# A fused cross-attention kernel: one operand sum moved from an accumulating DMA to VectorE, and operand loads asked for in another half of the period

## The chip, the cores and the metric

The kernel runs on one core of one Trainium2 chip. The time is the device time of one execution in microseconds (us); the median over executions is what counts. Everything is float32.

## The reference

For each of 8 batches, with `x1` and `x2` (the context) of 512 channels by 1024 positions:

```
q = x1^T Wq + bq          # 1024 x 64
k = Wk x2 + bk            # 64 x 1024
v = Wv x2 + bv            # 512 x 1024
attn = softmax(q k, over the 1024 context positions)
out = v attn^T + x1       # 512 x 1024
```

## The kernel before

**The algebra.** The kernel computes `out = Wv (x2 attn^T) + bv + x1`: it first forms `y = x2 E` with E the exponentials of the scores, then `o = Wv y`. Both products are done by a seven-product (Strassen-Winograd) scheme over 2 x 2 blocks. The left blocks of `y` are A11, A12, A21, A22 (`s.a["11"]` and so on: 128 partitions x 4 x 256, 512 KB each, loaded from a transposed copy of `x2`). Their sums are S1 = A21 + A22, S2 = A11 - S1, S3 = A11 - A21, S4 = A12 + S2. The right blocks are halves of E (`s.t["11"]` and so on, 128 x 4 x 512); T1 = E12 - E11, T2 = T1 - E22, T3 = E22 - E12, T4 = E21 + T2. The table `MULT` says which left and right operand product 1 to 7 takes: product 3 is S4 x E22, product 4 is A22 x T4, product 7 is S3 x T3. Some of these products are split once more by the same scheme: `inner_left` and `inner_right` make the inner sums on VectorE (lines 385 and 397), `inner_product` issues four 128x256 matmuls for each of the seven inner products (line 404).

**The stages.** The whole order is written by hand (`manual_schedule`): every engine and every DMA queue runs its instructions in the order of the Python program. `period(s, n, nn, nnn)` is called once for each batch b = 0 to 7 and is called "period b" here; `n`, `nn`, `nnn` are the next three batches. Its first half makes y of batch b: products 1, 2, 6, then the scores of `n` (first half of the positions) and the queries of `nn`, then products 5, 7, 3, the other scores of `n` and the keys of `nn`, and product 4. Its second half makes o of batch b (seven products against the weights) and, beside it on VectorE, the softmax of `n` and the sums S1, S2, S3 of `n`. Batches 2 to 7 are `late`; batches 2 to 5 and 7 (`seven`) split product 7 as well.

**How three sums are made in late periods.** VectorE makes T1 and T2 in two halves each. T3 (`sum_t3`) is made by ScalarE and DMA: ScalarE negates E12 in place (line 285), and an accumulating DMA on POOL's queue adds E22 (line 286), in two DMAs of 512 KB. T4 (`sum_t4`) is copied on ScalarE and accumulated by two DMAs of POOL's queue (line 280). S4 (`sum_s4`) is loaded again from A12's place in HBM by a DMA of SP's queue (line 291), and an accumulating DMA of POOL's queue adds S2 (line 292). POOL issues T3, T4 and S4 in that order, behind a partition all-reduce (line 226). S4 is read first by `inner_left(s, 3, ...)` on VectorE, which stands behind `inner_right(s, 7, ...)` (it reads T3) and, where there is a next batch, the four `lower` subtractions (line 249). In periods 0 and 1 VectorE makes S4 and T3 with `tensor_tensor`.

**Where loads stand.** `load_a` issues loads of A blocks on SP's queue; A11 and A12 have one buffer each, A21 and A22 two. S3 overwrites A21, and the inner sums of product 4 take A12's buffer (tag `a12`), those of the next batch's product 2 take S4's (tag `aS4`). In each period SP's queue has, in order: A11 of `n` (after product 1), S4's load, A21 and A22 of `n`, the four pieces of `x2` of `nn` (after the queries), the four of `x1` of `nnn` (after the keys), A12 of `n` (after product 4), and four stores of the output, each of which waits for an accumulating DMA of POOL's queue (line 569).

Of the kernel before, what the change touches and what calls it, by code (L numbers as in the profile page):

```python
# [9 lines left out]
F32 = mybir.dt.float32  # L10
AF = mybir.ActivationFunctionType
ALU = mybir.AluOpType
# [3 lines left out]
def kernel(  # L16
# [47 lines left out]
    nc = tc.nc  # L64
    P = 128
    B, C, N = x1.shape
# [3 lines left out]
    MH = N // P // 2  # L70
# [4 lines left out]
    sb = ctx.enter_context(tc.tile_pool(name="sb", bufs=1))  # L75
# [25 lines left out]
    def left_sums(a, *ks):  # L101

        for k in ks:
            x, y, op = {
                "S1": ("21", "22", ALU.add),
                "S2": ("11", "S1", ALU.subtract),
                "S3": ("11", "21", ALU.subtract),
                "S4": ("12", "S2", ALU.add),
            }[k]
            nc.vector.tensor_tensor(a["21" if k == "S3" else k], a[x], a[y], op)  # L110
            if k == "S3":
                a["S3"] = a["21"]
# [9 lines left out]
    def load_x(s, x):  # L122

        s.x = sb.tile([P, CT, N], F32, tag="x", name=f"x_{s.b}_{x.tensor.name}")
        for c in range(CT):
            nc.sync.dma_start(s.x[:, c, :], x[s.b, ts(c, P), :])

    def load_a(s, *ks):
        for k in ks:
            s.a[k] = sb.tile(  # L130
                [P, MH, C // 2], F32, tag=f"a{k}", name=f"a{k}_{s.b}", bufs=1 + (k[0] == "2")
            )
            nc.sync.dma_start(s.a[k], x2T[s.b, int(k[0]) - 1, int(k[1]) - 1])

    def sum_a(s, *ks):
        for k in ks:
            if k != "S3":
                s.a[k] = sb.tile([P, MH, C // 2], F32, tag=f"a{k}", name=f"a{k}_{s.b}")
        left_sums(s.a, *ks)

    def project(s, nm, w_sb, bank=None):

        if bank:
            ps = ps_a.tile([P, H], F32, tag=bank, name=f"ps_{nm}_{s.b}")
        else:
            ps = ps_s.tile([P, 2, H], F32, tag="sc", name=f"ps_{nm}_{s.b}")[:, 0, :]
        for c in range(CT):
            for h, r in ((0, lo), (1, hi)):
                nc.tensor.matmul(  # L149
                    ps[r, :],  # L150
                    w_sb[:, c, :],
                    s.x[:, c, ts(h, H)],
                    start=(c == 0),
                    stop=(c == CT - 1),
                )
        return ps
# [12 lines left out]
    def keys(s, bank=None):  # L169

        ps = project(s, "k", wk_sb, bank)
        s.k = sb.tile([P, H], F32, tag="k", name=f"k_{s.b}", bufs=2)
        nc.scalar.activation(s.k, ps, AF.Identity, bias=bk_sb)

    def scores(s, h, i, bank=None):


        if i == 0:
            s.e[h] = sb.tile([P, 2, MH, H], F32, tag=f"e{h}", name=f"e_{s.b}_{h}")
        e = s.e[h]  # L180
        if bank:
            whole = None
            ps = [
                ps_a.tile([P, H], F32, tag=f"{bank}{g}", name=f"ps_s{bank}{g}_{s.b}_{h}_{i}")
                for g in range(2)
            ]
        else:
            whole = ps_s.tile([P, 2, H], F32, tag="sc", name=f"ps_s_{s.b}_{h}_{i}")
            ps = [whole[:, g, :] for g in range(2)]
        for g, r in ((0, lo), (1, hi)):  # L190
            nc.tensor.matmul(  # L191
                ps[g], s.k[r, ts(i, P)], s.q[r, ts(h, H)], start=True, stop=True
            )

        def copy():
            if bank:
                for g in range(2):
                    nc.scalar.copy(e[:, g, i, :], ps[g])
            else:
                nc.scalar.copy(e[:, :, i, :], whole)  # L200

        copy.ps = ps
        return copy
# [19 lines left out]
    def total(s, h):  # L223
        fold_halves(s, h, ALU.add)
        s.den[h] = sb.tile([P, H], F32, tag="den", name=f"den_{s.b}_{h}", bufs=2)
        nc.gpsimd.partition_all_reduce(s.den[h], s.mx[h][:, 0, :], P, ReduceOp.add)  # L226
        s.few[h] = sb.tile([P, H // P], F32, tag="few", name=f"few_{s.b}_{h}", bufs=2)
        nc.gpsimd.dma_start(
            s.few[h], s.den[h][0:1, :].rearrange("o (p f) -> o p f", p=P)
        )  # L230
# [28 lines left out]
    def right_sums(t, k):  # L259

        x, y = {"T1": ("12", "11"), "T2": ("T1", "22"), "T3": ("22", "12"), "T4": ("21", "T2")}[k]
        nc.vector.tensor_tensor(t[k], t[x], t[y], ALU.add if k == "T4" else ALU.subtract)
# [8 lines left out]
    def sum_t4(s):  # L271

        s.t["T4"] = t4 = sb.tile([P, MH, H], F32, tag="eT4", name=f"eT4_{s.b}")
        if s.b < 2:
            sum_e(s, "T4")
            return
        for i in (0, 2):
            nc.scalar.copy(t4[:, i : i + 2, :], s.t["21"][:, i : i + 2, :])
        for i in (0, 2):
            nc.gpsimd.dma_start(t4[:, i : i + 2, :], s.t["T2"][:, i : i + 2, :], accum_op=ALU.add)  # L280

    def sum_t3(s, i):
# [1 line left out]
        t3 = s.t["T3"][:, i : i + 2, :]  # L284
        nc.scalar.mul(t3, t3, -1.0)
        nc.gpsimd.dma_start(t3, s.t["22"][:, i : i + 2, :], accum_op=ALU.add)

    def sum_s4(s):

        s.a["S4"] = sb.tile([P, MH, C // 2], F32, tag="aS4", name=f"aS4_{s.b}")  # L290
        nc.sync.dma_start(s.a["S4"], x2T[s.b, 0, 1])
        nc.gpsimd.dma_start(s.a["S4"], s.a["S2"], accum_op=ALU.add)

    def copy_u1(s, j):
        if j == 0:
# [3 lines left out]
    def sum_e(s, *ks, of=(0, 2)):  # L299
        for i in of:  # L300
            part = {n: v[:, i : i + 2, :] for n, v in s.t.items()}
            for k in ks:
                right_sums(part, k)
# [75 lines left out]
    def inner_left(s, i, x, tag):  # L379

        v = {f"{p + 1}{q + 1}": x[:, ts(q, MH // 2), ts(p, P)] for p in range(2) for q in range(2)}
        sums = sb.tile([P, 4, MH // 2, P], F32, tag=tag, name=f"aI{i}_{s.b}")
        for z, (k, x, y, op) in enumerate(LEFT):
            v[k] = sums[:, z]
            nc.vector.tensor_tensor(v[k], v[x], v[y], op)  # L385
        s.inner[i] = v
# [118 lines left out]
    def evict_y(s, k, steps=(1, 2)):  # L505

        bank, add = RESULT[k]
        rden = s.rden.get(int(k[1]) - 1)
        if 1 in steps:
            s.y[k] = sb.tile([P, 2, H], F32, tag=f"y{k}", name=f"y{k}_{s.b}")  # L510
        y = s.y[k]
        for step in steps:
            for j in range(2):
                if step == 1:
                    nc.vector.tensor_tensor(y[:, j, :], s.bank[bank, j], s.tmp[add][:, j, :], ALU.add)  # L515
                else:
                    nc.vector.tensor_tensor(y[:, j, :], y[:, j, :], rden, ALU.mult)  # L517
# [198 lines left out]
    def scores_and(n, h, bank, project):  # L716


        for i in range(MH):
            scores(n, h, i, bank if i == 2 else None)()  # L720
        project()
# [4 lines left out]
    def period(s, n, nn, nnn):  # L726
# [3 lines left out]
        late = s.b >= 2  # L730
        seven = late and (s.b < B - 2 or n is None)

        def first(i, hook=None):
            multiply(s, "y", i, s.a, s.t, MH, hook=hook)
# [24 lines left out]
        else:  # L759
            sum_e(s, "T1", "T2")  # L760
            total(s, 0)
        if n:
            load_a(n, "11")
        if s.b == 0:
            first(2)
            evict_y(s, "11", (1,))
            keys(n)
            load_x(nn, x1)
            sum_t4(s)
            sums(s, 1)  # L770
            shares(s, 0)
            sum_e(s, "T3")
        else:
            complete_2 = multiply_seeded(
                s,
                2,
                "y22",
                {5: lambda: copy_u1(s, 0), 4: lambda: copy_u1(s, 1)} if late else {},
            )
            if late:  # L780
                sum_t3(s, 0)
                sum_t3(s, 2)
            else:
                sums(s, 1)
            complete_2()
            evict_y(s, "11", (1,))
            if s.b == 1:
                shares(s, 0)
            sum_t4(s)
            if late:  # L790
                sum_s4(s)
            else:
                sum_a(s, "S4")
                sum_e(s, "T3")
        if n:
            load_a(n, "21", "22")
        first(6)
        if s.b == 1:
# [2 lines left out]
        if seven:  # L801
            inner_left(s, 7, s.a["S3"], "yT4")
        if late:
            inner_left(s, 4, s.a["22"], "a12")
            evict_y(s, "11", (2,))

# [73 lines left out]
        if s.b == 1:  # L880
            inner_left(s, 4, s.a["22"], "a12")
        if n:
            scores_and(n, 1, "a", nothing)
            if s.b == 0:
                exponential(n, 0, 0)
            if nn:
                next_keys()
# [12 lines left out]
            start_sum(n, 0)  # L900
        if n:
            load_a(n, "12")
        evict_y(s, "21")
        if s.b and n:
            total(n, 0)
# [80 lines left out]
```

## Time and profile before

| | |
|---|---|
| runs | 704.22, 706.20, 707.53 us; median 706.2 |
| the profiled execution | 712.57 us; span from first to last instruction 710.4 us |
| TensorE (PE) | busy 688.5 us, 2324 matmuls, mean granted clock 0.99 |
| VectorE (DVE) | busy 606.9 us |
| ScalarE (ACT) | busy 306.1 us |
| GpSimd (POOL) | busy 230.4 us |
| DMA | 121.62 MB; POOL's queue 45.69 MB (36.0% of 16 engines' span), SP's queue 73.28 MB (28.8%) |

In the timelines a line has start, duration, engine, source line, operation, output and inputs, and in brackets the time for which the engine sat idle before it and what ended that wait. `a`, `aS`, `aI` are blocks of A, their sums, and inner sums; `e`, `eT`, `eI7yT` are E, the T sums, and the right inner sums of product 7; `ps_i3third` is the PSUM tile of an inner product of product 3. T3 shows as `e<-e` where a DMA makes it, S4 as `aS<-aS`. The profiled execution took 6.4 us more than the median of the runs.

Periods overlap by design. The start of the keys' matmuls (line 149) marks them: 170.1 us in period 1, 260.0 in period 2, 345.2 in period 3, 431.2 in period 4, 517.9 in period 5. Period 6 has no such matmuls, and period 7 ends the program.

### The profile page before, as it was taken

How to read it: one execution, taken by the hardware profiler on the slowest of the kernel's cores; microseconds unless marked ns; L12 is line 12 of the kernel's file. 1: busy time of each engine (PE TensorE's matmuls, PEld its weight loads, DVE VectorE, ACT ScalarE, POOL GpSimd, SP SyncE). 2: the span in 40 equal slices, each digit the busy share in tenths (PEclk: the TensorE clock that was granted, in tenths of full speed). 3: DMA queues.
4: the chain of work that ended last, by engine and by line, in shares of the span. 5: the costliest groups of instructions: out<-in, count | busy, mean ns of one | idle time of the engine just before them, and what ended most of it. 6: DMA issues, size and time to landing. Idle time of an engine off the chain costs nothing.

```text
span 710.4 us, 6908 instructions
## 1 busy us (share of the span) xinstructions
PE 688.5 (97%) x2324; PEld 381.0 (54%) x2324; DVE 606.9 (85%) x788; ACT 306.1 (43%) x502; POOL 230.4 (32%) x165
## 2 busy tenths in 40 slices
PE   9999999999999899999999999999899999999897
PEld 5333554546464565646547465473654745564663
DVE  1999998987999598987899778997799968997584
ACT  2733344254436444365443553444535454434120
POOL 0133114512424216342272612725127242424100
PEclk9999999999999989999999999999999999999899
DMA  9676157856388963899619987189743895279603
GB/s 308 240 246 226 32 178 146 240 159 133 109 171 241 251 125 116 162 260 262 171 50 204 260 229 208 28 198 267 205 88 49 207 251 106 49 169 250 136 0 118
DMA packets 48179, 121.62 MB, mean 171 GB/s; under 512 B 5265, under 2 KB 7569, under 8 KB 48145
## 3 DMA queue, kind: packets, MB, share of 16 engines
q0 software_dynamic: 20016, 45.69, 36.0%
q1 hardware_dynamic: 26720, 73.28, 28.8%
q10 hardware_dynamic: 1408, 2.23, 0.9%
q8 instruction: 18, 0.29, 0.2%
q14 instruction: 17, 0.13, 0.1%
HBM read 75.76 MB, written 16.81 MB: 130 GB/s over the span
## 4 chain that ended last, share of the span: by engine, by line
PE 38%; DVE 29%; DMA 22%; POOL 5%; issue 4%; SPq 1%; ACT 0%; DVEq 0%; POOLq 0%
DMA aS<-aS 14%; PE ps_ya L340 6%; PE ps_oa L340 4%; DVE aI L385 3%; DMA row<-few 3%; DVE aS L110 3%; DVE e L249 3%; PE ps_oc L340 3%; PE ps_yc L404 3%; PE ps_k L149 3%; PE ps_i4chain L404 3%; PE ps_s L191 2%; POOL den L226 2%; PE ps_ya L404 2%; DVE uo L566 2%
## 5 line engine op out<-in xcount | busy, mean ns | idle before, releaser
L340 PE MATMUL ps_ya<-eT,aS 128*128 128x512 f32 x256 | 113.1, 595 | 0.0
L226 POOL PARTITION_ALL_REDUCE den<-sum x16 | 86.1, 5381 | 49.4 <-DVE sum L215 44.4
L340 PEld LDWEIGHTS ps_ya<-eT,aS 128*128 128x128 f32 x256 | 48.0, 190 | 60.9 <-issue 58.0
L249 DVE TENSOR_TENSOR e<-e,top 128x1024 f32<-128x1024 f32 x60 | 69.4, 1217 | 3.6 <-POOL top L221 3.6
L253 ACT ACTIVATE e<-e 128x1024 f32<-128x1024 f32 x60 | 62.4, 1059 | 18.8 <-DVE e L249 17.9
L221 POOL PARTITION_ALL_REDUCE top<-max x16 | 31.4, 1960 | 120.5 <-DVE max L215 71.0
L340 PE MATMUL ps_oa<-yT,w_S 128*128 128x512 f32 x128 | 57.6, 593 | 0.0
L200 ACT COPY e<-ps_s 128x1024 f32<-128x1024 f32 x46 | 45.6, 1026 | 19.1 <-PE ps_s L191 17.5
L351 ACT COPY uy<-ps_ya 128x512 f32<-128x512 f32 x36 | 21.0, 587 | 64.7 <-PE ps_ya L340 55.6
L191 PE MATMUL ps_s<-q,k 64*128 64x512 f32 x188 | 47.3, 608 | 0.8 <-ACT q L608 0.8
L238 POOL DMA_DIRECT2D den<-row x16 | 8.9, 559 | 119.7 <-DMA row<-few 119.7
L573 POOL DMA_DIRECT2D sum<-e x21 | 25.8, 1228 | 60.9 <-DMA sum<-e 20.4
L517 DVE TENSOR_TENSOR y<-y,den 128x512 f32<-128x512 f32 x64 | 40.3, 685 | 4.5 <-DMA den<-row 4.4
L340 PEld LDWEIGHTS ps_oa<-yT,w_S 128*128 128x128 f32 x128 | 24.2, 190 | 30.8 <-issue 29.2
L211 DVE TENSOR_TENSOR max<-max,e 128x1024 f32<-128x1024 f32 x30 | 36.7, 1225 | 3.0
L569 POOL DMA_DIRECT2D uo<-in_x_dram x14 | 16.5, 1176 | 54.9 <-DVE few L234 28.0
L351 ACT COPY uo<-ps_oa 128x512 f32<-128x512 f32 x32 | 18.4, 586 | 32.3 <-PE ps_oa L340 31.3
L515 DVE TENSOR_TENSOR y<-ps_yc,uy 128x512 f32<-128x512 f32 x48 | 30.7, 681 | 0.0
L191 PEld LDWEIGHTS ps_s<-q,k 64*128 64x128 f32 x188 | 16.7, 186 | 24.6 <-issue 18.4
L340 PE MATMUL ps_oa<-y,w_S 128*128 128x512 f32 (+1 forms) x68 | 28.8, 567 | 0.0
L360 PE MATMUL ps_o<-y,w 128*128 128x512 f32 x64 | 28.8, 592 | 0.0
L340 PE MATMUL ps_o<-y,w 128*128 128x512 f32 x64 | 28.8, 592 | 0.0
(175 smaller groups left out, 1424.4 us busy)
## 6 DMA issues: line engine op xcount, KB each, us to landing
x_in_x_dram<-in_x_dram SPq DMA_DIRECT2D x60, 512.0 KB, 7.0
a<-in_x2T_dram SPq DMA_DIRECT2D x32, 512.0 KB, 7.7
sum<-e POOLq DMA_DIRECT2D x21, 512.0 KB, 5.2
r<-in_x_dram POOLq DMA_DIRECT2D x14, 512.0 KB, 6.9
uo<-in_x_dram POOLq DMA_DIRECT2D x14, 512.0 KB, 7.7
out_dram<-r SPq DMA_DIRECT2D x14, 512.0 KB, 5.4
out_dram<-uo SPq DMA_DIRECT2D x14, 512.0 KB, 4.6
e<-e POOLq DMA_DIRECT2D x12, 512.0 KB, 8.6
```

The costliest lines, as they stand in the source:

```text
L191: nc.tensor.matmul(ps[g], s.k[r, ts(i, P)], s.q[r, ts(h, H)], start=True, stop=True)
L200: nc.scalar.copy(e[:, :, i, :], whole)
L211: nc.vector.tensor_tensor(f, e[:, :, 0, :] if i == 1 else f, e[:, :, i, :], op)
L221: nc.gpsimd.partition_all_reduce(s.top[h], s.mx[h][:, 0, :], P, ReduceOp.max)
L226: nc.gpsimd.partition_all_reduce(s.den[h], s.mx[h][:, 0, :], P, ReduceOp.add)
L249: nc.vector.tensor_tensor(e, e, top, ALU.subtract)
L253: nc.scalar.activation(e, e, AF.Exp)
L340: nc.tensor.matmul(ps[:, n], left[ka][:, k, ts(j, P)], right[kb][:, k, n], start=opens and k == 0, stop=i in (2, 3, 4) and k == n_k - 1, s ...
L351: nc.scalar.copy(s.tmp[i][:, j, :], ps)
L404: nc.tensor.matmul(ps, s.inner[i][ka][:, k, :], s.inner[i, "t"][kb][:, k, :], start=opens and k == 0, stop=z in (2, 3, 4) and k == MH // 2 ...
L515: nc.vector.tensor_tensor(y[:, j, :], s.bank[bank, j], s.tmp[add][:, j, :], ALU.add)
L517: nc.vector.tensor_tensor(y[:, j, :], y[:, j, :], rden, ALU.mult)
```

## The change

- In late periods VectorE makes S4 = A12 + S2 with one `tensor_tensor`, placed behind the left inner sums of product 7 and ahead of those of product 4. `sum_s4` goes, with its load on SP's queue and its accumulating DMA on POOL's.
- In period 7, T3 is made by VectorE in two `tensor_tensor` instructions, behind T4; its two ScalarE multiplications and two accumulating DMAs go. Periods 2 to 6 keep `sum_t3`.
- A11 of the next batch is loaded behind product 3's evictions, so behind the `x2` pieces in SP's queue, in periods 1 to 6. A21 and A22 are loaded at the end of product 4 for the batch after the next, behind A12 of the next; so A21 and A22 of batches 2 to 7 are asked for most of a period earlier. Period 0 still loads batch 1's blocks where it did.

```diff
@@ -284,12 +284,6 @@
-
-    def sum_s4(s):
-
-        s.a["S4"] = sb.tile([P, MH, C // 2], F32, tag="aS4", name=f"aS4_{s.b}")
-        nc.sync.dma_start(s.a["S4"], x2T[s.b, 0, 1])
-        nc.gpsimd.dma_start(s.a["S4"], s.a["S2"], accum_op=ALU.add)
@@ -759,9 +753,8 @@
             sum_e(s, "T1", "T2")
             total(s, 0)
-        if n:
+        if s.b == 0:
             load_a(n, "11")
-        if s.b == 0:
             first(2)
@@ -777,22 +770,21 @@
-            if late:
+            if late and n:
                 sum_t3(s, 0)
                 sum_t3(s, 2)
-            else:
+            elif not late:
                 sums(s, 1)
             complete_2()
             evict_y(s, "11", (1,))
             if s.b == 1:
                 shares(s, 0)
             sum_t4(s)
-            if late:
-                sum_s4(s)
-            else:
+            if not late:
                 sum_a(s, "S4")
+            if not late or n is None:
                 sum_e(s, "T3")
-        if n:
+        if s.b == 0:
             load_a(n, "21", "22")
         first(6)
@@ -801,6 +793,7 @@
         if seven:
             inner_left(s, 7, s.a["S3"], "yT4")
         if late:
+            sum_a(s, "S4")
             inner_left(s, 4, s.a["22"], "a12")
             evict_y(s, "11", (2,))
@@ -880,6 +873,8 @@
         if n:
+            if s.b:
+                load_a(n, "11")
             scores_and(n, 1, "a", nothing)
@@ -900,6 +895,8 @@
         if n:
             load_a(n, "12")
+        if nn:
+            load_a(nn, "21", "22")
         evict_y(s, "21")
```

## The prediction

> **What bounds the kernel now.** I read the page, then VectorE's waits, then the timelines around them. TensorE is busy for 97% of the span, so the gain to be had lies in its few idle or slow microseconds. The page's engine shares, and the chain of work that ended last:
>
> ```profile
> PE 688.5 (97%) x2324; PEld 381.0 (54%) x2324; DVE 606.9 (85%) x788; ACT 306.1 (43%) x502; POOL 230.4 (32%) x165
> ...
> PE 38%; DVE 29%; DMA 22%; POOL 5%; issue 4%; SPq 1%; ACT 0%; DVEq 0%; POOLq 0%
> DMA aS<-aS 14%; PE ps_ya L340 6%; PE ps_oa L340 4%; DVE aI L385 3%; DMA row<-few 3%; DVE aS L110 3%; DVE e L249 3%; PE ps_oc L340 3%; PE ps_yc L404 3%; PE ps_k L149 3%; PE ps_i4chain L404 3%; PE ps_s L191 2%; POOL den L226 2%; PE ps_ya L404 2%; DVE uo L566 2%
> ```
>
> The largest piece of the chain is S4's accumulating DMA. VectorE's waits (total, times, longest) name it too, and behind it T3's:
>
> ```profile
> DVE aI L385 <- DMA aS<-aS: 23.5, 6, 4.7
> ...
> DVE eI7yT L397 <- DMA e<-e: 12.0, 5, 5.4
> ```
>
> Period 4 on VectorE: T3 ends a wait of 1.45 us, the four subtractions run, and S4 ends a wait of 3.73 us.
>
> ```profile
> 407.38 1.30 DVE L397 TENSOR_TENSOR eI7yT<-e 128x512 f32<-128x512 f32 x2 [1.45 <-DMA e<-e]
> 408.71 0.69 DVE L397 TENSOR_TENSOR eI7yT<-eI7yT,e 128x512 f32<-128x512 f32 x1
> 409.44 0.69 DVE L397 TENSOR_TENSOR eI7yT<-e,eI7yT 128x512 f32<-128x512 f32 x1
> 410.05 4.62 DVE L249 TENSOR_TENSOR e<-e,top 128x1024 f32<-128x1024 f32 x4
> 418.40 0.76 DVE L385 TENSOR_TENSOR aI<-aS 128x256 f32<-128x256 f32 x2 [3.73 <-DMA aS<-aS]
> ```
>
> TensorE in period 2: short waits at product 3, after which four matmuls take 1.9 to 2.05 us, where others take 1.03.
>
> ```profile
> 245.64 1.13 PE L404 MATMUL ps_i3chain<-e,aS 128*128 128x256 f32 x4 [1.54 <-DMA aS<-aS]
> 248.04 2.05 PE L404 MATMUL ps_i3third<-eI3eT,aI 128*128 128x256 f32 x4 [1.28 <-DVE eI3eT L397]
> 249.88 1.91 PE L404 MATMUL ps_i3chain<-eI3eT,aI 128*128 128x256 f32 x4
> ```
>
> By stretch, the granted clock (the number after the engines) is half after those waits, and again in period 7:
>
> ```profile
> 245.64:247.50 1.86, 1.13 (x4) 0.67 (x4) 1.79 (x5) 0.37 (x1) 1.17 (x2) 0.94 0.19 75
> 247.50:254.70 7.20, 6.66 (x17) 5.41 (x18) 6.76 (x11) 1.70 (x3) 1.82 (x2) 0.54 0.55 112
> ...
> 661.40:667.00 5.60, 5.49 (x13) 4.43 (x14) 2.04 (x4) 0.73 (x2) 0.00 (x0) 0.50 1.06 211
> ```
>
> **How much TensorE loses there.** Undisturbed, product 7 takes 6.04 us (327.03 to 333.07) and product 3 with the scores takes 9.77 us (period 1, 160.32 to 170.09): 15.81 from product 7 to the keys. Measured: period 2 22.94 (237.09 to 260.03), 3 18.12, 4 19.00, 5 19.70. Lost: 7.13, 2.31, 3.19, 3.89. Period 6: product 3 to product 4 11.92 against 9.77, product 4 6.57 against 6.14: 2.58. Period 7: product 5's last matmul could end at 656.49, product 4 starts at 676.33: 19.84 against 12.08: 7.76. Sum 26.9 us. Elsewhere from 85 us on, TensorE's timeline has no gap, so 26.9 is the ceiling of a gain.
>
> **The change, part by part.**
>
> *S4 by VectorE, +6 instructions.* A 128x1024 sum is 1.22 us (line 110): 7.3 us more on VectorE. It stands where VectorE next waits anyway: period 3 idles 0.15 (row 517) and 2.08 (for the scores, row 211) directly behind, period 4 2.16, period 5 1.07 and 0.64, period 6 2.45 and 0.47. Period 2 has 0.69, but then 2.81 for T3. Queued behind S4 are product 4's left sums (read 20 us later), the divisions at line 517 and the maxima. Cost on the path: 0; with the cover gone 1.22 each. A sum beside an all-reduce took 3.15 us (line 110 at 281.79), so a bad place costs 1.93 more. In period 6 S4 comes beside the all-reduce; there two left sums already take 2.15 us (elsewhere 0.75), so the cost only moves to S4, and 2.9 us of idling follow. [...]
>
> *What goes.* Six loads on SP (0.66 us each to issue) and six accumulating DMAs on POOL (0.95 us, 18.2 us to landing), 6 MB with their reads. A12 is on chip since the period before, S2 too, so nothing new is waited for. The 23.5 us of VectorE waiting go.
>
> *What is late next.* In period 4 the subtractions end at 414.67. Left sums of S4 1.63, right sums of E22 2.65: 418.95, where product 3 begins at 418.2 and needs the first right sum at 419.06 (it is there at 416.9). Lines 447, 515 and product 4's right sums (0.6, 1.2, 2.6) end at 423.5; product 3's copies are there at 423.3, product 3 ends at 424.25, line 498 at 425.6, and the scores need the bank at 426.2. So the stall goes, with 0.6 us to spare, even if T3 lands no earlier. Period 5 gives 0.7 by the same sum, period 3 1.2, period 2 up to 1 us short.
>
> *T3's wait (12.0 us).* T3 and T4 on POOL's queue now share the engines with four 512 KB loads that SP issues at 306 to 308 (period 3). All four leave this place. T3's landing (8.6 us median) should fall; bounds are 7.3 (fastest row) and today's 10.3 (slowest). I take no gain, since the slack above doesn't need one.
>
> *Moved loads.* Each issue takes 0.33 to 0.42 us of SP, which idles for tens of us at line 570. A21 and A22 follow A12 at 355 us, with buffers free as product 4 has ended; the DMA engines are idle soon after (their busy tenths in slices of 1 us from 345):
>
> ```profile
> DMA  0069999989896000000000000012799999959899
> ```
>
> That is 13 empty slices, 358 to 371 us, and A12's 512 KB landed in 3.3 us just ahead: the 1 MB fits in. A21 and A22 are first read some 95 us later. A11 goes out behind `x2` at about 325 and is read at 366.9 (S2); the slowest landing of a block was 10.8. In a full stretch (DMA share 1.05, 276 GB/s) its 0.5 MB takes 1.9 us from T4 and the row of denominators, which lost 2.5 MB of rivals ahead. Cost 0; bounds 0 and 1.9 per period. The stores wait for nothing new.
>
> *T3 of period 7 by VectorE.* Two sums, 2.45 us; two multiplications (2.1 us of ScalarE) and two DMAs (8.6 us) go. VectorE: line 515 ends 648.25, T3 650.7, left sums of product 7 652.8, S4 654.0, left sums of product 4 655.6, line 517 656.8, reciprocal 656.9. Right sums of product 7 then give T3's at 657.55 and T2's at 658.9, wanted at 657.4 and 658.4. Loss 0.6, taken as 1.0 in place of 7.76; bounds 0 and 3.67 (2.45 + 1.22).
>
> **The sum.** Left over: period 2 0.5 (a ScalarE copy now late by 0.53), periods 3 to 5 0.2 each, period 6 0.4 (its scores' copies), period 7 1.0: 2.5. Gain 26.9 - 2.5 = 24.4: the profiled execution would take 712.57 - 24.4 = 688.2. It is 6.4 above the median of 706.2. If those 6.4 are the same waits, larger under the profiler, TensorE's work stays and the median after is also 688.2; if they lie elsewhere, it is 681.8. I take the middle, **685 us**.
>
> The half clock is worth 5.8 of the 26.9 (6.7 groups of four at 1.71 instead of 0.86). The rows show it after single waits of 1.3 to 2.1 us. [...]
>
> **The rivals.**
>
> - *T3 takes S4's place in periods 2 and 7.* VectorE waited longest for T3 there (2.81 and 5.40), and the clock halved there. If period 2 keeps its 7.13 and period 7 loses 6.5 (3.67 of VectorE on the path and 2.8 of slow clock), the gain is 24.4 - 6.6 - 5.5 = 12.3: 694 to 700 by the two readings of the 6.4, middle 697. Against it: T3 of period 7 is ready by 650.7, six us ahead of product 7.
> - *Hidden anyway: 706.* The 2.5 MB taken from the DMA engines free nothing and VectorE fills its idle time with other waits of the same length (for ScalarE's copies, 11.3 us at line 478). Against it: those lie behind product 3 and shrink with it.
> - *Slower: VectorE becomes the bound.* It is busy 75 to 76 us of the 85 to 87 of a period, and afterwards 77 of 83. Place: between T3's landing and product 3. If every added sum lies on the path and no stall goes, 706.2 + 7.3 + 2.45 = 716; with the 1.93 on each of eight, 731. It decides once T3 lands some 4.5 us later than now (0.6 to spare, 3.2 of stall regained, 0.6 per period for half a percent). A11 in the full stretch, or POOL held up while VectorE sums, could do that. Against it: T3's DMAs are issued before A11, and all their rivals left.
>
> **How the numbers follow.** Half a percent, 3.5 us, is about what a measurement tells from no change. Forecast 0.74 (its own range 679 to 690), T3 in S4's place 0.13, hidden 0.05, slower 0.08. Faster: 0.74 + 0.13. The range starts at 677 (the whole 26.9 off the fastest run, 704.2) and ends at 699, past the first rival's middle; above it lie some 0.04 of that rival and the last two, 0.17 in all.
>
> **What would show it.** Right: no `aS<-aS`; product 7 to the keys within 16.5 us in periods 2 to 5; the granted clock at 1.00 throughout; line 385's wait gone; T3's landing at or below 8.6 us. Wrong: the wait at `eI7yT` over 4 us, a wait of S2 (line 110) for A11, a longer wait of line 351 for stores, or TensorE waiting on VectorE at other lines.

## The result and the profile after

The kernel after takes 686.98 us in the median of four runs (686.32 to 687.60), the kernel before 705.67 (four runs beside it, 704.22 to 707.53): a ratio of 0.9734, 95% interval 0.9707 to 0.9760. The forecast was 685, with 677 to 699 as its range. The profiled execution after took 686.51 us (span 684.7); against the 712.57 of before that is 26.1 us less, where the working had 24.4, with 26.9 as the ceiling. By the medians, 705.67 and 686.98, the gain is 18.7 us: the profiled execution of before was a slow one.

The lines from 291 on that are cited here are lower by 6 in the kernel after: line 404 of before is 398 here, 397 is 391, 385 is 379, 441 is 435.

The page of after, with the engines' shares and the chain of work that ended last:

```profile
PE 677.9 (99%) x2324; PEld 378.3 (55%) x2324; DVE 617.2 (90%) x796; ACT 303.6 (44%) x500; POOL 211.5 (31%) x157
...
PE 94%; DMA 4%; SPq 1%; ACT 1%; DVE 1%; issue 0%; DVEq 0%
```

The chain had 38% TensorE, 29% VectorE and 22% DMA; it is now TensorE nearly alone. TensorE's busy time fell by 10.6 us at the same 2324 matmuls: they became shorter on the average. The half clock is 5.8 us of it (before has a clock of 0.50 from 247.29 to 254.11 and from 660.31 to 667.12, with 6.07 and 5.61 us of matmuls, half of which is lost: at the half clock groups of four matmuls begin 1.71 us apart, at full clock 0.86); the other 4.8 was not traced. TensorE's waits in after (total, times, longest); the first five lie before 85 us:

```profile
PE ps_warm L647 <- DVE warm L644: 1.0, 1, 1.0
PE ps_s L191 <- ACT q L602: 0.8, 1, 0.8
PE ps_k L149 <- DMA x_in_x_dram<-in_x_dram: 0.3, 1, 0.3
PE ps_q L598 <- DMA x_head<-in_x_dram: 0.3, 1, 0.3
PE ps_ya L334 <- ACT e L244: 0.3, 1, 0.3
PE ps_i4third L398 <- ACT e L200: 0.3, 1, 0.3
```

From 85 us to the end one wait of 0.3 us is left, in period 6. By stretch, from one period's keys to the next (periods 2 to 5; the columns are length, then busy time and instructions of PE, PEld, DVE, ACT and POOL, then the granted clock, the DMA share and GB/s):

```profile
170.31:253.12 82.81, 82.81 (x294) 48.11 (x292) 80.77 (x109) 40.34 (x68) 26.95 (x21) 1.00 0.72 175
253.12:336.18 83.06, 83.06 (x294) 47.96 (x292) 77.28 (x102) 40.23 (x68) 26.64 (x21) 1.00 0.74 181
336.18:419.17 82.99, 82.99 (x294) 47.95 (x292) 77.22 (x103) 40.23 (x68) 26.22 (x21) 1.00 0.75 183
419.17:501.99 82.82, 82.82 (x295) 48.11 (x293) 78.04 (x104) 40.45 (x68) 33.48 (x21) 1.00 0.74 179
```

Before, the same four stretches were 89.9, 85.1, 86.0 and 86.7 us. TensorE is now busy for all of each and its clock is full throughout.

VectorE in period 4, the place that the prediction showed of before:

```profile
389.57 1.22 DVE L110 TENSOR_TENSOR aS<-a,aS 128x1024 f32<-128x1024 f32 x1
...
398.67 1.83 DVE L391 TENSOR_TENSOR eI7yT<-e 128x512 f32<-128x512 f32 x2 [0.36 <-DMA e<-e]
400.54 0.69 DVE L391 TENSOR_TENSOR eI7yT<-eI7yT,e 128x512 f32<-128x512 f32 x1
401.26 0.69 DVE L391 TENSOR_TENSOR eI7yT<-e,eI7yT 128x512 f32<-128x512 f32 x1
401.87 4.62 DVE L249 TENSOR_TENSOR e<-e,top 128x1024 f32<-128x1024 f32 x4
406.41 0.75 DVE L379 TENSOR_TENSOR aI<-aS 128x256 f32<-128x256 f32 x2
```

S4 is made at 389.57 in 1.22 us. T3 ends a wait of 0.36 us, not 1.45, and the left sums of S4 follow the subtractions with no wait, where they had waited 3.73.

DMA issues on POOL's queue (how many, KB each, median us from issue to landing): T3 (`e<-e`), T4 (`eT<-eT`) and S4 (`aS<-aS`) before, then T4 and T3 after:

```profile
e<-e POOLq DMA_DIRECT2D x12, 512.0 KB, 8.6
eT<-eT POOLq DMA_DIRECT2D x12, 512.0 KB, 13.4
aS<-aS POOLq DMA_DIRECT2D x6, 512.0 KB, 18.2
```

```profile
eT<-eT POOLq DMA_DIRECT2D x12, 512.0 KB, 9.4
e<-e POOLq DMA_DIRECT2D x10, 512.0 KB, 6.0
```

Period 7 on VectorE, with T3 and S4 made there:

```profile
629.69 2.84 DVE L262 TENSOR_TENSOR e<-e 128x1024 f32<-128x1024 f32 x2
...
634.04 1.22 DVE L110 TENSOR_TENSOR aS<-a,aS 128x1024 f32<-128x1024 f32 x1
...
638.17 1.26 DVE L391 TENSOR_TENSOR eI7yT<-e 128x512 f32<-128x512 f32 x2
```

Product 7 begins at 638.60 on TensorE and product 4 at 650.74: 12.14 us, where undisturbed they are 12.08 apart.

### The profile page after: what moved, and what is told of

The parts are those of the page before. It is cut to its first block, busy times and chain, and to the rows that moved or that the text cites. A ratio compares the mean times of both kernels' runs of the same rounds, so it can differ in the third digit from the quotient of the medians.

```text
span 684.7 us, 6896 instructions
## 1 busy us (share of the span) xinstructions
PE 677.9 (99%) x2324; PEld 378.3 (55%) x2324; DVE 617.2 (90%) x796; ACT 303.6 (44%) x500; POOL 211.5 (31%) x157
## 4 chain that ended last, share of the span: by engine, by line
PE 94%; DMA 4%; SPq 1%; ACT 1%; DVE 1%; issue 0%; DVEq 0%
PE ps_ya L334 18%; PE ps_oa L334 12%; PE ps_oc L334 8%; PE ps_yc L398 8%; PE ps_s L191 6%; PE ps_ya L398 5%; PE ps_o L334 4%; PE ps_o L354 4%; PE ps_q L149 4%; PE ps_k L149 3%; PE ps_i4chain L398 3%; PE ps_i3chain L398 3%; PE ps_yc L334 3%; PE ps_i2chain L398 3%; PE ps_i1chain L398 2%; PE ps_i7chain L398 2%
## 5 line engine op out<-in xcount | busy, mean ns | idle before, releaser
L226 POOL PARTITION_ALL_REDUCE den<-sum x16 | 72.6, 4536 | 58.0 <-DVE sum L215 53.2
L345 ACT COPY uo<-ps_oa 128x512 f32<-128x512 f32 x32 | 18.2, 588 | 28.0 <-PE ps_oa L334 28.0
L191 PEld LDWEIGHTS ps_s<-q,k 64*128 64x128 f32 x188 | 16.7, 186 | 24.7 <-issue 18.2
L334 PE MATMUL ps_oc<-y,w 128*128 128x512 f32 x64 | 28.8, 592 | 0.0
L334 PE MATMUL ps_o<-y,w 128*128 128x512 f32 x64 | 28.8, 592 | 0.0
```

Of the source, the lines that this page charges most:

```text
L191: nc.tensor.matmul(ps[g], s.k[r, ts(i, P)], s.q[r, ts(h, H)], start=True, stop=True)
L334: nc.tensor.matmul(ps[:, n], left[ka][:, k, ts(j, P)], right[kb][:, k, n], start=opens and k == 0, stop=i in (2, 3, 4) and k == n_k - 1, s ...
L345: nc.scalar.copy(s.tmp[i][:, j, :], ps)
```

## The experiments

Each kernel was timed beside runs of the kernel before on the same chip, whose medians were 707.64 for the first four, 708.97 for the next four and 707.20 for the last three. Periods are named as above; a period without loss is 82.8 us from keys to keys. The kernel after was timed beside the 705.67 alone. The same kernel before differs by 3.3 us from one group to another, and the ratios of the kernels with two S4 sums, with the unread DMA and with the split alone (0.9720 to 0.9727) lie within the interval of after; so what these lose against it is read from the traces.

| kernel | us, lowest to highest | ratio to before, 95% |
|---|---|---|
| S4 alone | 690.54 (688.92 to 691.08) | 0.9746 (0.9721 to 0.9771) |
| moved loads alone | 701.45 (701.05 to 701.81) | 0.9903 (0.9881 to 0.9926) |
| T3 of period 7 alone | 702.26 (699.43 to 704.02) | 0.9913 (0.9881 to 0.9945) |
| S4 and T3, loads unmoved | 686.63 (686.29 to 687.48) | 0.9695 (0.9668 to 0.9723) |
| after, S4 made twice | 689.43 (688.33 to 691.97) | 0.9720 (0.9703 to 0.9736) |
| after, S4 made four times | 700.10 (698.81 to 700.86) | 0.9873 (0.9857 to 0.9889) |
| after, unread S4 DMA put back | 689.32 (687.50 to 691.14) | 0.9723 (0.9701 to 0.9745) |
| after, product 7 split in period 6 | 689.57 (689.24 to 689.95) | 0.9727 (0.9712 to 0.9741) |
| after, exponentials later | 688.01 (687.11 to 688.35) | 0.9738 (0.9713 to 0.9762) |
| S4 four times, exponentials later | 699.18 (698.37 to 699.98) | 0.9898 (0.9872 to 0.9923) |
| product 7 split, exponentials later | 689.87 (688.37 to 691.53) | 0.9767 (0.9740 to 0.9794) |

### One part at a time

**S4 by VectorE alone** (made from before):

```diff
-            if late:
-                sum_s4(s)
-            else:
+            if not late:
                 sum_a(s, "S4")
...
         if late:
+            sum_a(s, "S4")
             inner_left(s, 4, s.a["22"], "a12")
```

> S4 by VectorE alone; the loads stay where they were, T3 of period 7 stays with ScalarE and DMA. Theory (S4's landing was the wait, and the 0.6 us to spare behind T3 doesn't need lighter DMA engines): TensorE's losses of periods 2 to 6 go, 1 to 2 us of 19 stay; period 7 still waits for T3 and loses 6 to 7 of its 7.8. So 692 to 695 us against 705.7 before and 687.0 with the whole change. Rival (the crowd of loads in front of T3 makes everything late, and T3's wait takes S4's place): T3's landing stays at 8.6 us, VectorE's wait for T3 grows in every period, 698 to 702 us.

Measured 690.54. The keys start at 170.12, 252.94, 335.99, 418.80 and 501.62: periods 2 to 5 take 82.8, 83.1, 82.8 and 82.8 us, with the loads unmoved. What is left is period 7, where ScalarE and DMA still make T3 (TensorE's timeline):

```profile
641.35 1.13 PE L404 MATMUL ps_i7third<-eI7yT,aI 128*128 128x256 f32 x4 [2.10 <-DVE eI7yT L397]
642.77 2.04 PE L404 MATMUL ps_i7chain<-eI7yT,aI 128*128 128x256 f32 x4 [0.28 <-DVE eI7yT L397]
```

Product 7 takes 10.46 us there (638.23 to 648.69) in place of 6.04. So S4's DMA was the whole stall in periods 2 to 5, the half clock of period 2 included, and T3's landing was no second wall behind it: the first rival falls for period 2, and the third (VectorE the bound) falls. The first rival is right about period 7 taken alone, and the T3 part of the change is what removes it.

**The moved loads alone** (A11 behind product 3, A21 and A22 behind A12, made from before):

```diff
-        if n:
-            load_a(n, "11")
         if s.b == 0:
+            load_a(n, "11")
...
-        if n:
+        if s.b == 0:
             load_a(n, "21", "22")
...
+            if s.b:
+                load_a(n, "11")
             scores_and(n, 1, "a", nothing)
...
+        if nn:
+            load_a(nn, "21", "22")
```

> The loads moved alone; S4 is still loaded again and accumulated by DMA. Theory: with three loads gone from in front, T4's landing falls from 13.4 to about 10 us as in the changed kernel, and S4's, behind it in the same queue, by the same 4 us from 18.2 to about 14; the wait at S4's left sums (3.4 to 4.7 us) shrinks to under 1.5, and most of the losses of periods 2 to 6 go here too; period 7 has no such loads and keeps its 7.8: 694 to 698 us. Rival (the accumulating DMA itself is slow, whatever runs beside it): S4's landing stays above 17 us, the wait stays, 703 to 706 us.

A miss: 701.45, between the expected 694 to 698 and the rival's 703 to 706, and S4's landing hardly moved, as the rival had it. The DMA issues of this kernel:

```profile
e<-e POOLq DMA_DIRECT2D x12, 512.0 KB, 6.7
eT<-eT POOLq DMA_DIRECT2D x12, 512.0 KB, 10.8
aS<-in_x2T_dram SPq DMA_DIRECT2D x6, 512.0 KB, 4.8
aS<-aS POOLq DMA_DIRECT2D x6, 512.0 KB, 17.1
```

Without the rival loads T3 lands 1.9 us earlier, T4 2.6 and S4's plain load 2.6, but S4's accumulating DMA only 1.1, and VectorE still waits 16.7 us for it in all. The expectation had it fall by 4. What the rows show is that S4, the last of five accumulating DMAs on POOL's queue, lands last with those loads beside it (18.2 us) and without them (17.1); why it takes about 6 us more than T4 ahead of it wasn't tried, nor was S4 issued ahead of the others.

**T3 of period 7 alone** (made from before):

```diff
-            if late:
+            if late and n:
                 sum_t3(s, 0)
                 sum_t3(s, 2)
-            else:
+            elif not late:
                 sums(s, 1)
...
+            if not late or n is None:
                 sum_e(s, "T3")
```

> T3 of period 7 by VectorE alone. Theory: periods 0 to 6 unchanged; in period 7 the 1.6 and 2.1 us waits of product 7 and the half clock go, S4's DMA still ends about 10 us after its load, now with two DMAs less ahead of it: period 7 regains 5 to 7 us: 699 to 701 us. Rival (in period 7 S4 is what is waited for, T3 only stands ahead of it): 1 us or less, 704 to 706 us.

Measured 702.26, a little over what was expected. Product 7 to product 4 in period 7 is 14.92 us (651.46 to 666.38), 19.85 before: 4.9 regained, and the rest is S4's DMA, which product 3 now waits for. T3's landing elsewhere stays at 8.6 and S4's at 18.0.

**S4 and T3 with the loads left where they were** (the change without its `load_a` lines):

> S4 and T3 by VectorE, the loads left in the first half of the period: the whole change without its moved loads. Theory: the loads add nothing once S4 is off the queue: 687 to 688.5 us, T3's landing near 8 us with VectorE waiting 0.5 to 2 us for it and TensorE not at all. Rival (moving the loads is worth several us by itself): 690 us or more, with waits of TensorE at products 7 and 3.

As expected: 686.63, no more than the whole change takes. From 85 us on TensorE has two waits of 0.3 us, both for ScalarE's line 200; T3 lands in 6.5 us and T4 in 9.9. Once S4 is off the queue the moved loads are worth nothing that these runs can tell, though by themselves, with S4 still on the queue, they were worth 6.2.

### How much room VectorE has left

The prediction's slower rival was VectorE as the bound, with "0.6 us to spare". Two kernels repeat the sum of S4 (the result is the same, the extra sums are redone work), each adding 1.22 us of VectorE per repeat in periods 2 to 7.

```diff
             sum_a(s, "S4")
+            left_sums(s.a, "S4")
```

> The changed kernel with S4's sum made twice in each late period: 1.22 us more of VectorE at the same place, no other work. Theory (S4 fits into VectorE's idle time with some 0.5 us to spare): of the second 1.22 us, periods 2 to 5 put 0.5 to 1.1 us each on TensorE's path, at product 3 and the scores behind it, period 6 nothing (it idles 2.66 and 1.83 us there), period 7 about 0.5: 689 to 691.5 us against 687.0. Rival (VectorE has microseconds to spare): 686.5 to 687.8 us.

```diff
             sum_a(s, "S4")
+            left_sums(s.a, "S4", "S4", "S4")
```

> The changed kernel with S4's sum made four times in each late period: 3.66 us more of VectorE. Theory: beyond the first half microsecond every added one counts, 3 to 3.5 us in each of periods 2 to 5, 0 to 1 in period 6, 2.5 to 3.5 in period 7: 14 to 18 us, so 701 to 705 us, with granted clocks below 1.00 only if waits of over 2 us come close together. Rival (several us to spare): under 698 us.

Made twice, the time is in the expected range, but not for the expected reason: periods 2, 4 and 5 lose nothing or 0.3 (83.10, 82.82, 82.81), period 3 loses 4.4 (87.22), and period 7 1.3 (13.41 us from product 7 to product 4, 12.14 in after). The profiled execution is the slowest of the four, 691.97 us with a mean clock of 0.998; the other three took 688.33 to 689.93 at a clock of 1.00, so they had no half clock, and the loss of period 3 is not one of every execution. ScalarE there, and TensorE behind it:

```profile
322.80 1.06 ACT L253 ACTIVATE e<-e 128x1024 f32<-128x1024 f32 x1 [4.88 <-DVE e L249]
323.76 0.57 ACT L345 COPY uy<-ps_ya 128x512 f32<-128x512 f32 x1
324.23 0.38 ACT L435 COPY ps_yc<-ps_i7chain 128x256 f32<-128x256 f32 x1
```

```profile
324.65 1.13 PE L398 MATMUL ps_i7chain<-eI7yT,aI 128*128 128x256 f32 x4 [2.20 <-ACT ps_yc L435]
325.62 1.55 PE L398 MATMUL ps_yc<-e,a 128*128 128x256 f32 x4
326.96 1.91 PE L398 MATMUL ps_i7chain<-eI7yT,aI 128*128 128x256 f32 x4
```

The first exponential of the next scores stands ahead of two PSUM copies in ScalarE's order. It waits for VectorE's subtractions; when those are late it holds up the copies, and TensorE waits for the second of them. The wait of 2.20 us is followed by matmuls at half clock, from 325.99 to 329.40; these 3.41 us at half speed (groups of four 1.71 us apart in place of 0.86) cost another 1.7. Why it was period 3 that was late enough was not tried.

Made four times, the time is 700.10, a little under the expected 701 to 705 and over the rival's 698. The periods are 87.28, 84.10, 84.10 and 84.09. Of 3.66 us added, a steady period loses 1.3, so VectorE had about 2.4 us to spare there. The only wait that VectorE shows in period 4 is then 1.4 us, at line 472; in after it waits 4.2 us in three places (2.4, 1.4 and 0.4). In period 7, where TensorE waits 3.71 us for the right sums, product 7 takes 11.7 us in place of 6.04. The clock fell after one wait each time, 2.52 us in period 2 and 3.71 in period 7, where the expectation had it only if waits of over 2 us came close together.

**Is it the order on ScalarE?** In the kernel after, and in the one with four sums, the first exponential was moved behind product 7's first copy, and what follows it one hook later each:

```diff
-                        1: lambda: copy_first(n, 0),
-                        6: lambda: add_exponential(1),
-                        5: lambda: add_exponential(2),
+                        1: lambda: exponential(n, 0, 0),
+                        6: lambda: copy_first(n, 0),
+                        5: lambda: add_exponential(1),
+                        4: lambda: add_exponential(2),
...
-            first(5, (lambda: exponential(n, 0, 0)) if n else None)
+            first(5)
```

> The changed kernel, with the first exponential of the next scores moved on ScalarE from product 5's first copy to product 7's first copy, and the copy and exponentials behind it one hook later each. Theory (TensorE bounds the changed kernel and ScalarE's queue only has room to spare at product 7): no time moves, 686 to 687.5, periods 82.8 to 83.1. Rival (the later exponentials make the sum over the softmax late, and with it the all-reduce behind it): 688 to 691, with a longer wait of VectorE for the sum tile.

> Four S4 sums in each late period, with the same move of the exponentials. Theory (the extra VectorE work reached TensorE through ScalarE's queue, where exponential 0 waits for the subtractions ahead of the copies of products 5 and 7): the wait of 1.01 us at product 7's chain in periods 3 to 5 and the 2.52 us in period 2, with the half clock, go; 3 x 1.3 + 4.5 = 8.4 of the 13 us lost are regained, 691 to 694; period 7's 5 us stay. Rival (VectorE itself is the bound by then, and the wait comes back at the next thing it makes): 698 to 701.

The second was the test, and the theory failed in the steady periods. TensorE with four sums, order as in after:

```profile
411.79 1.13 PE L398 MATMUL ps_i7chain<-eI7yT,aI 128*128 128x256 f32 x4 [1.01 <-ACT ps_yc L435]
```

and with the exponential later:

```profile
414.97 1.10 PE L398 MATMUL ps_i3chain<-eI3eT,aI 128*128 128x256 f32 x4 [0.17 <-DVE eI3eT L391]
422.06 1.13 PE L191 MATMUL ps_sa<-q,k 64*128 64x512 f32 x4 [0.61 <-DVE y L492]
```

The wait at product 7 is gone, and two others have come, at product 3 and at the scores behind line 492 (line 498 of before). The period is 84.10 in both, and in both VectorE is busy for 81.0 us of it, with one wait, 1.4 us at line 472. So at that load VectorE sets the period, as far as these two kernels show, and the order on ScalarE only decides where TensorE meets it. Period 2 is the exception: it fell from 87.28 to 85.61, since the single wait of 2.52 us with its half clock became four of 0.23 to 0.61 at full clock; VectorE shows no wait in it and is busy for 83.9 us. By the whole time, 699.18 against 700.10 on another chip, the two can't be told apart.

In the kernel after, the move brings nothing: 688.01, over the expected 686 to 687.5 and at the rival's 688. Its periods 3 and 4 are 83.58 and 83.56, half a microsecond longer than in after; in the whole run VectorE waits 7.6 us for the softmax sum's tile, 4.7 in after, as the rival had it.

### Does the DMA traffic matter by itself?

Three quarters of S4's old traffic were put back into after: a load and an accumulating DMA into a tile that nothing reads.

```diff
+            if late:
+                shadow = sb.tile([P, 3, C // 2], F32, tag="shadow", name=f"shadow_{s.b}")
+                nc.sync.dma_start(shadow, x2T[s.b, 0, 1][:, 0:3])
+                nc.gpsimd.dma_start(shadow, s.a["S2"][:, 0:3], accum_op=ALU.add)
```

> The changed kernel with three quarters of the old S4 traffic put back beside it: a load on SP's queue and an accumulating DMA on POOL's into a tile that nobody reads. VectorE still makes the S4 that is used. Theory (the wait counted, not the traffic): T3's landing rises from 6.0 to some 7 to 8 us, VectorE waits up to 1.5 us for it, TensorE under 0.5 per period: 687 to 688.5 us. Rival (the traffic itself held things up): 691 us or more, with TensorE waiting at products 7 and 3.

Between the two: 689.32. Its DMA issues:

```profile
eT<-eT POOLq DMA_DIRECT2D x12, 512.0 KB, 10.0
e<-e POOLq DMA_DIRECT2D x10, 512.0 KB, 5.9
...
shadow<-aS POOLq DMA_DIRECT2D x6, 384.0 KB, 17.2
```

The unread DMA lands nearly as late as S4's did (17.2 us), T3 lands as early as without it, and T4 0.6 us later. TensorE never waits at product 7 or 3. So it was the waiting for S4 that cost at products 7 and 3, not its bytes. The loss that there is lies mostly in the second half of a period: from keys 419.89 to 504.53 the stretch is 84.64 us (82.82 in after), where VectorE waits 4.2 us for the softmax sum's accumulating DMA and TensorE then 0.37 and 0.50 us for evictions. In all VectorE waits 9.0 us for that tile, 4.7 in after.

### Is there more to be had in period 6?

In after, period 6 is the one late period in which product 7 isn't split. The split saves a product 0.86 us of TensorE.

```diff
-        seven = late and (s.b < B - 2 or n is None)
+        seven = late
```

> The changed kernel with product 7 split in period 6 too, as in the other late periods: TensorE does 0.9 us less (6.04 in place of 6.9), VectorE 5 us more, where it idles 2.66 and 1.83 us now. Theory (TensorE is the bound and VectorE has this room in period 6): 686.0 to 687.0 us, within 0.5% of the changed kernel. Rival (VectorE becomes the bound there): 688 to 690 us.

> Product 7 split in period 6 too, with the same move of the exponentials. Theory (the split failed in period 6 because of exponential 0 ahead of the copies): no wait of 1.98 us at product 7 in period 6, no half clock there; product 7 as split products takes 6.04 us in place of 6.9, so 685.7 to 686.8, at or up to 0.9 us below the changed kernel. Rival (VectorE is late in period 6 whatever the order on ScalarE): 688 to 690, with TensorE waiting at product 7 or 3 of period 6.

Neither pays, as the rivals had it: 689.57 and 689.87. From the keys of period 5 to product 4 of period 6 after takes 80.05 us, the split alone 83.15, and the split with the exponential later 81.47. With the split alone TensorE waits for the copy behind the exponential, as with two sums in period 3, and then runs at half clock for 3.41 us, to 572.36:

```profile
568.89 2.05 PE L398 MATMUL ps_i7chain<-eI7yT,aI 128*128 128x256 f32 x4 [1.98 <-ACT ps_yc L435]
```

With the exponential later, this wait and the half clock are gone and three waits on VectorE come:

```profile
573.38 1.10 PE L398 MATMUL ps_i3third<-eI3eT,aI 128*128 128x256 f32 x4 [0.34 <-DVE eI3eT L391]
574.71 1.10 PE L398 MATMUL ps_i3chain<-eI3eT,aI 128*128 128x256 f32 x4 [0.23 <-DVE eI3eT L391]
581.79 1.13 PE L191 MATMUL ps_sa<-q,k 64*128 64x512 f32 x4 [0.61 <-DVE y L492]
```

Product 3 to product 4 is then 11.71 us, 9.77 in after: what the split saves is lost to VectorE, and more. No kernel tried is clearly faster than the changed one; the one with the loads unmoved (686.63) can't be told from it.

## Why the prediction was right, point by point

- **S4's landing is the stall, and it goes.** Shown: S4 alone brings periods 2 to 5 to 82.8 to 83.1 us.
- **S4 costs nothing on VectorE.** Shown for the five periods 2 to 5 and 7: 1.22 us each, in idle time. In period 6, beside the all-reduce (549.18 to 552.41 on POOL), it took 1.70 us: 0.48 more, where 1.93 was the bound from the 3.15 us row. When the sum began (550.80), 1.61 us of the all-reduce were left by the profile; in the 3.15 us row 3.06 were left (281.79 to 284.85).
- **T3's landing, "I take no gain".** Mis-sized: 8.6 us fell to 6.0. The runs show two causes of about one size, each enough for most of it: 6.9 with S4 alone, 6.7 with the loads alone. How S4's going does it is open: with three quarters of its traffic put back T3 still lands after 5.9.
- **"0.6 us to spare".** Mis-sized for the kernel as it is: some 2.4 us per steady period by the four sums. Much of the difference may be the T3 that lands 2.6 us earlier, which the step left out on purpose. In period 7 there was none: a second sum cost 1.3 us. The place was partly wrong too: beside line 498 and the scores, which showed up with the exponential later, the first to suffer is a copy in ScalarE's order at product 7, which the step did not look at.
- **Moved loads at 0.** Right, shown by the kernel without them.
- **T3 of period 7, 1.0 lost of 7.76.** Mis-sized: 0.06. VectorE's line 515 (509 after) ended 8.8 us ahead of product 7, where the step had 8.2 (648.25 to 656.49), and the missing 0.6 us was about the loss it worked out. The two sums themselves took 2.84 us, not 2.45.
- **Left over, 2.5 us in all.** Against the undisturbed lengths after loses 0.0, 0.25, 0.2 and 0.0 in periods 2 to 5, 0.56 in period 6 and 0.06 in period 7: 1.1 in place of 2.5. These 1.4 us are most of the 1.7 by which the sum's gain of 24.4 fell short of the 26.1 measured.
- **The 6.4 us between the profiled execution and the median.** The middle was the wrong choice and makes the forecast 2.0 us low. The first reading fits: the profiled execution of after (686.51) agrees with its median (686.98), TensorE is busy for 99% of it, and the sum's 688.2 was the better forecast. A second profile shows where most of the 6.4 us of before lay. Up to period 6 the kernel with T3 of period 7 alone is the kernel before; from the keys of period 1 to product 4 of period 6 its profiled execution took 424.3 us (170.77 to 595.04) and that of before 430.0 (170.09 to 600.06), where after takes 411.7. So 5.7 us differ between two executions of the same code, on two chips, in the stretch whose losses the change removes.
- **The half clock goes with the waits.** Right: from 85 us on the clock of after is 1.00, up to its last microsecond. That the clock falls "after single waits of 1.3 to 2.1 us" was misread: in before it fell within the second of two waits (at 247.29 in the 1.28 us that end at 248.04, behind 1.54; at 660.31 in the 2.12 us that end at 661.51, behind 1.61), and single waits of 1.28 us in period 5 and 1.18 in period 6 were not followed by it. The price of 5.8 us, read from the rows, held.

The rivals: T3 in S4's place (694 to 700) is refuted by the kernel with S4 alone in period 2, and removed in period 7 by the third part of the change. Hidden anyway (706) is refuted by the result. VectorE as the bound is a real limit, but in a steady period it lies about 2.4 us of work further off. Of POOL held up while VectorE sums, before shows this: the first all-reduce of line 226 takes 10.95 us in periods 2 to 5 (at 273.90 with the sum of 3.15 us beside it), and elsewhere from 85 us on that line takes 3.19 to 4.14; what holds it was not tried.

## What to carry to other kernels

In this kernel the transfer at the end of an accumulating queue was dear by when it landed (18.2 us after its issue), not by its bytes: an operand that costs one 1.22 us vector instruction was better made there, as that engine still idled a few microseconds per period at the right place. How much it idles can be measured by doing a known piece of its work twice and four times: in periods 4 and 5 here the first 1.22 us were free, and of 3.66 us 1.3 were lost. Where a wait lowered the clock the loss was larger than what was added (4.4 us for 1.22 in period 3). And when a profiled execution is slower than the median of the runs, build the forecast from the work of the engine that will be the bound, not from the middle of two readings.

## What the runs showed of the hardware

- TensorE's granted clock stood at half for 3.41 us at a time (568.95 to 572.36 with the split, 325.99 to 329.40 with two S4 sums, 419.11 to 422.51 with T3 of period 7 alone), or for 6.8 us (twice in before). It fell after single waits of 1.98, 2.20, 2.52 and 3.71 us, but the length of one wait does not decide. With T3 of period 7 alone the waits of period 4 are 0.63 and 1.28 us, 1.13 apart, and the clock falls; in period 5 of before they are 0.76 and 1.28, as far apart, and it stays full. TensorE's idle time is the first number less the second, and the granted clock is the third from the end; the first two lines are of T3 alone, the others of before:

```profile
415.70:419.10 3.40, 1.66 (x7) 1.19 (x8) 2.85 (x7) 0.37 (x1) 1.80 (x2) 1.00 0.43 153
419.11:422.51 3.40, 3.40 (x9) 2.46 (x8) 3.37 (x6) 0.90 (x3) 0.00 (x0) 0.50 0.95 172
503.29:506.70 3.41, 2.20 (x9) 1.27 (x8) 1.53 (x5) 1.35 (x3) 0.88 (x2) 1.00 0.88 330
506.70:510.11 3.41, 2.36 (x10) 1.83 (x11) 3.34 (x7) 0.49 (x2) 0.92 (x1) 1.00 0.86 180
```

  The idle time is 1.74 us in the 3.40 us ahead of the fall with T3 alone, and 1.21 and 1.05 us in the two stretches of before that no fall followed. The half clock set in inside a wait in before (247.29 and 660.31, in waits that end at 248.04 and 661.51) and after one with T3 alone (419.11, where the wait ends at 418.57). What decides it was not shown. The periods with waits of 2.20 and 2.52 us lost 4.4 and 4.5 us in all.
- In these runs a 512 KB accumulating DMA has landed 5.8 to 8.6 us after its issue in the median when it stands first or second on POOL's queue (T3), after 9.4 to 13.4 us as third or fourth (T4), and after 17.1 to 18.2 us as fifth (S4, and the unread one of 384 KB): S4 18.2 in before, 17.1 with the plain loads beside it moved away, the unread one 17.2.
